# Seven block products for eight in the r and z gates, and partial results seeded into PSUM

## The chip, the core and the metric

The kernel runs on one core of one Trainium2 chip. The metric is device time in microseconds, first to last instruction, as a median of several executions. The kernel works in float32. In this kernel's trace every float32 product appears as two matmul entries, so a count in the trace is twice the count in the code.

## The reference

64 graphs of 256 nodes with 256 features; `x` and `adj` are both (64, 256, 256). Cut to what matters:

```python
h = maximum(layernorm(x), 0)
out = x + layer(h, adj)

# layer(x, mask), d = 256
xc = transpose(x)
c = relu(bn(conv1d(xc, conv1_w)))                  # 1 tap
c = bn(conv1d(c, conv2_w, pad=8))                  # 17 taps
x_conv = transpose(relu(c + xc))
s = x @ w_se.T + b_se                              # 3 features
A = exp(-dist(s)) * mask
msg = relu(x @ w_msg.T + b_msg)
x_nmp = einsum('bnm,bmd->bnd', A, msg)
gi = concat([x_conv, x_nmp]) @ w_ih.T + b_ih       # 512 -> 3 * 256
gh = x @ w_hh.T + b_hh                             # 256 -> 3 * 256
r = sigmoid(gi_r + gh_r)
z = sigmoid(gi_z + gh_z)
n = tanh(gi_n + r * gh_n)
return (1 - z) * n + z * x
```

## The kernel before

Everything is kept transposed (channels on partitions). Two graphs form a *pair* (index `i`, 512 columns: two graphs of 256 nodes), four pairs form a *batch* of eight graphs. conv2 is done for a whole batch at once by a polynomial transform of length 16 along the nodes: VectorE makes the forward transform (`U`, `V`), TensorE multiplies each of 16 bins with its transformed filter (15 of them complex, three real products each), VectorE transforms back (`Yu`, `Yv`). The bins' filters are streamed from DRAM, 256 KB for each product. The rest is done pair by pair and is interleaved by hand; a small model (`pace`) decides where queued VectorE steps are put.

Tiles in PSUM, and one step of conv2 (two bins):

```python
def aux(): return psum.tile([P, W], FP, name="aux", bufs=3)     # W = 512: one bank
def acc(): return psum.tile([P, W], FP, name="acc", bufs=5)

def products(b, m, between=None):
    p = [acc() for _ in range(3)]
    for n in range(2):
        if n and between: between()
        for kind, v in enumerate(operands(2 * m + n)):
            ...                                   # 4 matmuls of 128 columns into p[kind]
            load_kind(b, 2 * m + n + 3, kind)     # filter, three bins ahead, 9 buffers
    p1 = work.tile([P, W], FP, name="p1")
    if m < 7:
        nc.scalar.copy(p1, p[0])
        nc.vector.tensor_sub(re, pv[0], pv[2])    # pv[0] is p1
        nc.vector.tensor_add(im, pv[0], pv[1])
    ...
```

From the features to the weighted adjacency of a pair:

```python
def message(i):
    for g in range(G):
        for c in range(MC):
            p = acc() if g * MC + c == 3 else aux()
            ...                                               # 2 matmuls of 259 columns
            nc.vector.tensor_add(MSG[i][:, g, c, :], p[:, :D + SE], b_msg)
    ...                                                       # ScalarE: four small ops into z
    for g in range(G):
        nc.scalar.activation(MSG[i][:, g, :, :D], MSG[i][:, g, :, :D], AF.Relu)

def embed(i):                                                 # z is transposed
    p = aux()
    for j in range(2):
        transpose(p[:, j * P:(j + 1) * P], Z[:, j].rearrange("p q s -> p (q s)"))
    nc.scalar.copy(ZT[:, :P], p[:, :P])
    ...                                                       # and eight copies of 32 x 128

def affinity(i):                                              # exp(-dist) * adj
    for g in range(G):
        for c in range(MC):
            p = acc() if q == 3 else aux()
            nc.tensor.matmul(p[:, :N], ZT[rows_q, :P], ZT[rows_q, P:], start=True, stop=True)
            nc.scalar.activation(E[i][:, g, c], p[:, :N], AF.Exp, scale=-1.0)
    ...                                                       # four VectorE products with adj
```

The gates, called twice for each pair (`dc` is the half of the 256 output channels):

```python
def gates(i, dc, wait=None, early=None):
    ...
    ghn = acc()
    product(ghn, h, n, True, True)
    nc.scalar.activation(gn, ghn, AF.Identity, bias=...)
    pr, pn, pz = acc(), acc(), acc()
    product(pr, h + xn, r, True, False)          # h: the pair itself, xn: aggregated messages
    if early: early()
    product(pn, xn, n, True, False)
    product(pz, h + xn, z, True, False)
    if wait: wait()
    product(pr, xc, r, False, True)              # xc: the convolution's result
    nc.scalar.activation(tr, pr, AF.Tanh, ...)
    nc.vector.scalar_tensor_tensor(gn, tr, 1.0, gn, op0=ALU.add, op1=ALU.mult)
    product(pn, xc, n, False, True)
    nc.vector.scalar_tensor_tensor(gn, gn, 0.5, pn, op0=ALU.mult, op1=ALU.add)
    nc.scalar.activation(nn, gn, AF.Tanh, ...)
    product(pz, xc, z, False, True)
    nc.scalar.activation(tz, pz, AF.Tanh, ...)
    ...                                          # three VectorE steps: (1 - z) * n + z * h into d
```

Each `product` is two or four matmuls of 512 columns. `finish(i)` transposes `d` back, adds `x` and stores. The schedule of a batch, cut:

```python
    message(i); products(b, 0); embed(i); products(b, 1); affinity(i); products(b, 2)
    finish(i - 1); products(b, 3); aggregate(i); products(b, 4)
    message(i + 1)
    products(b, 5, lambda i=i: embed(i + 1))
    affinity(i + 1)
    join_h(nxt)                     # nxt: the same pair of the next batch; two ScalarE copies
    products(b, 6); products(b, 7)
    aggregate(i + 1)
    message(i + 2)
    gates(i, 0, wait, early)        # early: embed(i + 2); wait: affinity(i + 2), conv1(nxt)
    gates(i, 1, None, early)        # early: join_h(nxt + 1)
    conv1(nxt + 1); aggregate(i + 2)
    gates(i + 1, 0, lambda nxt=nxt: join_h(nxt + 2))
    conv1(nxt + 2); finish(i)
    gates(i + 1, 1)
    join_h(nxt + 3); message(i + 3); conv1(nxt + 3)
    gates(i + 2, 0, wait, lambda i=i: embed(i + 3))
    aggregate(i + 3); finish(i + 1)
    gates(i + 2, 1)
    gates(i + 3, 0); finish(i + 2); gates(i + 3, 1)
```

Of the kernel before, what the change touches and what calls it, by code (L numbers as in the profile page):

```python
# [42 lines left out]
class Fft:  # L43
# [160 lines left out]
    def p_back(self, Y, T):  # L204


        return [self.sub(T(0, 0), Y(0, 4), Y(1, 4)),
                self.sub(T(0, 2, 2), Y(0, 6, 2), Y(1, 6, 2)),
                self.add(Y(0, 4), Y(0, 4), Y(1, 4)),
# [71 lines left out]
def filter_points(bins, taps):  # L281


    cols = []
    for n in bins:
        z = [(ROOTS[n] if n < 15 else 1.0) ** (taps - 1 - t) for t in range(taps)]
        if n < 15:
            cols += [[v.real for v in z], [v.imag - v.real for v in z], [v.real + v.imag for v in z]]
        else:
            cols += [[1.0] * taps, [(-1.0) ** (taps - 1 - t) for t in range(taps)]]  # L290
    return np.array(cols, np.float64).T
# [10 lines left out]
def kernel(  # L302
# [221 lines left out]
    def aux():  # L524
        return psum.tile([P, W], FP, name="aux", bufs=3)

    def acc():
        return psum.tile([P, W], FP, name="acc", bufs=5)
# [5 lines left out]
    def columns(name):  # L534
        t, n = ROWS[name]
        k = sum(n)
        p = aux()
        nc.tensor.transpose(p[:, :k], t, ident[:k, :k])
        c = const.tile([P, k], FP, name=f"{name}_columns")
        nc.vector.tensor_copy(c, p[:, :k])  # L540
        return [c[:, sum(n[:j]):sum(n[:j + 1])] for j in range(len(n))]
# [80 lines left out]
    def transpose_h(i):  # L622
        if i >= B // G:
            return
        HT[i] = work.tile([P, DC, W], FP, name="hT", bufs=6)
        for dc in range(DC):
            p = aux()
            for j in range(G * MC):
                transpose(chunk(p, j // MC, j % MC), X[i][:, j, dc * P:(dc + 1) * P])
            if i == 0:  # L630
                nc.vector.tensor_scalar(HT[i][:, dc, :], p, 0.0, None, ALU.max)
            else:
                nc.scalar.activation(HT[i][:, dc, :], p, AF.Relu)  # L633
# [41 lines left out]
    def conv1(i, other=acc):  # L675
        if i >= B // G:
            return
        for o in range(DC):
            p = acc() if o == 0 else other()
            for k in range(DC):  # L680
                mm(p, w_c1[:, k, o * P:(o + 1) * P], HT[i][:, k, :], W, start=(k == 0), stop=(k == DC - 1))
            v = h1.rearrange("p (g o) s b -> p o g s b", o=DC)[:, o, :, :, 1:1 + NW]
            u = p.rearrange("p (g s b) -> p g s b", g=G, b=NW)
# [23 lines left out]
    def filters(m, g, eng):  # L707
# [3 lines left out]
        p = acc()  # L711
        for dc in range(DC):
            mm(p[:size * kinds, dc * D:(dc + 1) * D], points[m][:size * TAPS, :size * kinds],
               taps[:size * TAPS, g, dc, :], D, start=True, stop=True)
# [6 lines left out]
    WB = {}  # L721

    def load_kind(b, n, kind):
        b, n = b + n // BINS, n % BINS
        if b < NB and (n < BINS - 1 or kind < 2):
            WB[b, n, kind] = work.tile([P, DC, D], FP, name="wb", bufs=9)
            m = n // len(PASSES[0])
            nc.sync.dma_start(out=WB[b, n, kind], in_=filt[m][:, 3 * (n - PASSES[m][0]) + kind])  # L728

# [14 lines left out]
    def products(b, m, between=None):  # L744
        p = [acc() for _ in range(3)]
        for n in range(2):
            if n and between:
                between()
            for kind, v in enumerate(operands(2 * m + n)):
                if v is None:  # L750
                    load_kind(b, 2 * m + n + 3, kind)
                    continue
                for o in range(DC):
                    for k in range(DC):
                        mm(p[kind][:, (n * DC + o) * P:(n * DC + o + 1) * P],
                           WB[b, 2 * m + n, kind][:, k, o * P:(o + 1) * P],
                           v[:, k::DC, 0, :], P, start=(k == 0), stop=(k == DC - 1))
                load_kind(b, 2 * m + n + 3, kind)
        p1 = work.tile([P, W], FP, name="p1")
        pv = [t.rearrange("p (n a e) -> p a n e", n=2, e=NW) for t in (p1, p[1], p[2])]  # L760
        if m < 7:
            nc.scalar.copy(p1, p[0])
            if m < 4:
                re, im = Yv(m % 2, m // 2 * 2, 2), Yv(m % 2, 4 + m // 2 * 2, 2)
            elif m < 6:
                re, im = Yu(m - 4, 0, 2), Yu(m - 4, 2, 2)
            else:
                t = Yu.t[:, :, :, 6:8, :].rearrange("p a c n e -> p n a c e")
                re, im = t[:, 0], t[:, 1]
            pace.vector(2 * W, pace.pe + PSUM)  # L770
            nc.vector.tensor_sub(re, pv[0], pv[2])
            nc.vector.tensor_add(im, pv[0], pv[1])
        else:
            half = W // 2
            nc.scalar.copy(p1[:, :half], p[0][:, :half])
            nc.scalar.mul(Yu(0, 4)[:, :, 0, :], p[0][:, half:].rearrange("p (a e) -> p a e", e=NW), 0.5)
            nc.scalar.mul(Yu(1, 4)[:, :, 0, :], p[1][:, half:].rearrange("p (a e) -> p a e", e=NW), 0.5)
            pace.vector(W, pace.pe + PSUM)
            nc.vector.tensor_sub(Yu(0, 5)[:, :, 0], pv[0][:, :, 0], pv[2][:, :, 0])
            nc.vector.tensor_add(Yu(1, 5)[:, :, 0], pv[0][:, :, 0], pv[1][:, :, 0])  # L780
# [11 lines left out]
    def message(i):  # L792
        MSG[i] = work.tile([P, G, MC, D + SE], FP, name="msg")
        for g in range(G):
            for c in range(MC):
                p = acc() if g * MC + c == 3 else aux()
                for k in range(DC):
                    mm(p[:, :D + SE], chunk(HT[i][:, k], g, c), w_msg[:, k, :], D + SE,
                       start=(k == 0), stop=(k == DC - 1))
                pace.vector(D, pace.pe + PSUM)  # L800
                nc.vector.tensor_add(MSG[i][:, g, c, :], p[:, :D + SE], b_msg)
# [11 lines left out]
    def embed(i):  # L813
        p = aux()
        for j in range(2):
            transpose(p[:, j * P:(j + 1) * P], Z[:, j].rearrange("p q s -> p (q s)"))
        nc.scalar.copy(ZT[:, :P], p[:, :P])
        for q in range(G * MC):
            for c in range(MC):
                m = q // MC * MC + c  # L820
                nc.scalar.copy(ZT[q * Q:(q + 1) * Q, (1 + c) * P:(2 + c) * P], p[m * Q:(m + 1) * Q, P:2 * P])


    def affinity(i):
        E[i] = work.tile([P, G, MC, N], FP, name="e")
        for g in range(G):
            for c in range(MC):
                q = g * MC + c
                p = acc() if q == 3 else aux()
                rows_q = slice(q * Q, q * Q + KD)  # L830
                nc.tensor.matmul(p[:, :N], ZT[rows_q, :P], ZT[rows_q, P:], start=True, stop=True)  # L831
                nc.scalar.activation(E[i][:, g, c], p[:, :N], AF.Exp, scale=-1.0)
# [10 lines left out]
    def transpose_a(i):  # L843
        AT[i] = late.tile([P, 2 * MC, W], U16, name="adjh").bitcast(FP).rearrange("p a (b n) -> p a b n", n=N)
        AT[i] = AT[i].rearrange("p a b n -> p (a b) n").rearrange("p (g c) n -> p g c n", g=G)
        for g in range(G):
            q = aux()
            for c in range(MC):
                for r in range(MC):
                    transpose(q[:, c * N + r * P:c * N + (r + 1) * P], E[i][:, g, r, c * P:(c + 1) * P])  # L850
            nc.scalar.copy(AT[i][:, g].rearrange("p c n -> p (c n)"), q)

    def aggregate(i):
        XNM[i] = late.tile([P, DC, W], FP, name="xnm", bufs=2)
        for dc in range(DC):
            p = aux()
            for g in range(G):
                for c in range(MC):
                    mm(graph(p, g), MSG[i][:, g, c, dc * P:(dc + 1) * P], AT[i][:, g, c, :], N,
                       start=(c == 0), stop=(c == MC - 1))  # L860
            nc.scalar.activation(XNM[i][:, dc, :], p, AF.Copy)
# [3 lines left out]
    OT = {}  # L865

    def gates(i, dc, wait=None, early=None):
        h = [(w_hh[:, k], HT[i][:, k, :]) for k in range(DC)]
        xn = [(w_ih[:, DC + k], XNM[i][:, k, :]) for k in range(DC)]
        xc = [(w_ih[:, k], xcv(i % PB, k)) for k in range(DC)]  # L870

        def product(p, terms, row, first, last):
            for j, (w, r) in enumerate(terms):
                mm(p, w[:, row:row + P], r, W, start=first and j == 0, stop=last and j == len(terms) - 1)

        r, z, n = dc * P, D + dc * P, 2 * D + dc * P
        ghn = acc()
        product(ghn, h, n, True, True)
        gn = late.tile([P, W], FP, name="gn")
        nc.scalar.activation(gn, ghn, AF.Identity, bias=b_hh[:, 2 * DC + dc:2 * DC + dc + 1])  # L880
        pr, pn, pz = acc(), acc(), acc()
        product(pr, h + xn, r, True, False)
        if early:
            early()
        product(pn, xn, n, True, False)
        product(pz, h + xn, z, True, False)
        if wait:
            wait()
        product(pr, xc, r, False, True)
        tr = late.tile([P, W], FP, name="tr")  # L890
        nc.scalar.activation(tr, pr, AF.Tanh, bias=b_rz[:, dc:dc + 1], scale=0.5)  # L891
        pace.vector(W, pace.pe + ACT)
        nc.vector.scalar_tensor_tensor(gn, tr, 1.0, gn, op0=ALU.add, op1=ALU.mult)  # L893
        product(pn, xc, n, False, True)
        pace.vector(W, pace.pe + PSUM)
        nc.vector.scalar_tensor_tensor(gn, gn, 0.5, pn, op0=ALU.mult, op1=ALU.add)  # L896
        nn = late.tile([P, W], FP, name="nn")
        nc.scalar.activation(nn, gn, AF.Tanh, bias=b_ih[:, 2 * DC + dc:2 * DC + dc + 1])  # L898
# [286 lines left out]
```

## Time and profile before

| what | value |
|---|---|
| time, median of 3 | 1829.45 us (1827.57 to 1829.56) |
| gate matmuls with xnm, hT and Yv, 128x512 | 3 x 768 entries |
| conv2's matmuls, 128x128, with V, U, Sv, PT | 1024, 1024, 512 and 448 entries |
| VectorE subtract and add of conv2 (L771, L772, 128x512) | 22.0 + 21.8 + 16.4 + 16.4 us |
| ScalarE copy p<-acc (L762) | 32.9 us, 587 ns each |
| mean granted TensorE clock | 0.995 |

How to read the profile: PE is TensorE's matmuls and PEld its weight loads, DVE is VectorE, ACT is ScalarE, POOL is GpSimd. A line `DVE gn L893 <- ACT tr L891: 209.5, 34, 11.9` says that VectorE sat idle before line 893 until ScalarE's line 891 was done, 209.5 us in 34 times, at most 11.9 at once. The chain of work that ended last goes back from the last instruction, at each step to what released it. In a timeline, an entry gives start, length, engine, line, operation and count, and in brackets the idle time before it. Idle time of an engine that isn't the bottleneck costs nothing.

### The profile page before, as it was taken

How to read it: one execution, taken by the hardware profiler on the slowest of the kernel's cores; microseconds unless marked ns; L12 is line 12 of the kernel's file. 1: busy time of each engine (PE TensorE's matmuls, PEld its weight loads, DVE VectorE, ACT ScalarE, POOL GpSimd, SP SyncE). 2: the span in 40 equal slices, each digit the busy share in tenths (PEclk: the TensorE clock that was granted, in tenths of full speed). 3: DMA queues.
4: the chain of work that ended last, by engine and by line, in shares of the span. 5: the costliest groups of instructions: out<-in, count | busy, mean ns of one | idle time of the engine just before them, and what ended most of it. 6: DMA issues, size and time to landing. Idle time of an engine off the chain costs nothing.

```text
span 1828.3 us, 21930 instructions
## 1 busy us (share of the span) xinstructions
PE 1793.1 (98%) x7462; PEld 1110.8 (61%) x7462; DVE 1366.6 (75%) x2596; ACT 765.4 (42%) x1508; POOL 219.2 (12%) x357
## 2 busy tenths in 40 slices
PE   5999999999999999999999999999999999999998
PEld 3787454964569544784448645595546944487453
DVE  4789669794879849797697967888587984979422
ACT  2535532364333643265422653246432463225321
POOL 2211002101111011111012000110111110111000
PEclk9999999999999999999999999999999999999999
DMA  7788543854438444565347644494544744164011
GB/s 195 230 272 216 125 105 88 242 144 114 109 95 258 101 106 93 154 198 116 84 99 215 171 91 110 86 263 119 114 102 118 224 106 95 42 185 116 8 40 34
DMA packets 250483, 245.96 MB, mean 135 GB/s; under 512 B 142936, under 2 KB 176500, under 8 KB 250371
## 3 DMA queue, kind: packets, MB, share of 16 engines
q1 hardware_dynamic: 216634, 183.83, 37.0%
q0 software_dynamic: 30784, 58.07, 14.1%
q10 hardware_dynamic: 2953, 2.66, 0.7%
q8 instruction: 59, 0.97, 0.2%
q14 instruction: 53, 0.43, 0.1%
HBM read 156.56 MB, written 44.30 MB: 110 GB/s over the span
## 4 chain that ended last, share of the span: by engine, by line
PE 94%; issue 2%; DMA 2%; DVE 1%; POOL 1%; ACT 0%; SPq 0%; POOLq 0%; ACTq 0%
PE acc L517 80%; PE aux L517 11%; PE aux L521 2%; PE aux L831 1%; DMA x<-in_x_dram 1%; DMA filt<-fo 1%; DMA wb<-filt 0%; POOL filt L717 0%; POOL rstd L565 0%; DVE st L559 0%; ACT fo L716 0%; SPq L728 0%; POOL bn_scale L595 0%; DVE Sv L571 0%; DVE y L926 0%
## 5 line engine op out<-in xcount | busy, mean ns | idle before, releaser
L517 PE MATMUL acc<-xnm,w_ih 128*128 128x512 f32 x768 | 353.1, 592 | 0.0
L517 PE MATMUL acc<-hT,w_hh 128*128 128x512 f32 x768 | 350.5, 592 | 0.0
L517 PE MATMUL acc<-Yv,w_ih 128*128 128x512 f32 x768 | 342.7, 596 | 1.9 <-ACT Yv L789 1.9
L517 PEld LDWEIGHTS acc<-Yv,w_ih 128*128 128x128 f32 x768 | 145.8, 191 | 185.4 <-issue 180.9
L517 PEld LDWEIGHTS acc<-xnm,w_ih 128*128 128x128 f32 x768 | 144.7, 190 | 176.0 <-issue 175.5
L517 PEld LDWEIGHTS acc<-hT,w_hh 128*128 128x128 f32 x768 | 143.9, 190 | 164.6 <-issue 152.6
L893 DVE SCALAR_TENSOR_TENSOR gn<-tr,gn 128x512 f32<-128x512 f32 x64 | 44.1, 689 | 209.6 <-ACT tr L891 209.5
L891 ACT ACTIVATE tr<-acc,b_rz 128x512 f32<-128x512 f32 x64 | 43.9, 686 | 344.6 <-PE acc L517 344.6
L927 POOL DMA_DIRECT2D out_dram<-y x62 | 38.3, 622 | 785.0 <-DVE y L926 760.0
L517 PE MATMUL acc<-V,wb 128*128 128x128 f32 x1024 | 124.8, 275 | 0.0
L517 PE MATMUL acc<-U,wb 128*128 128x128 f32 x1024 | 124.3, 276 | 0.0
L517 PEld LDWEIGHTS acc<-U,wb 128*128 128x128 f32 x1024 | 120.0, 192 | 3.6 <-DVE T L59 2.0
L59 DVE SCALAR_TENSOR_TENSOR V<-T,V 128x256 f32<-128x256 f32 (+2 forms) x224 | 121.8, 613 | 0.3
L517 PEld LDWEIGHTS acc<-V,wb 128*128 128x128 f32 x1024 | 119.5, 192 | 0.0
L517 PE MATMUL acc<-hT,w_c 128*128 128x512 f32 x228 | 107.4, 612 | 2.3 <-ACT hT L633 1.4
L517 PE MATMUL aux<-e,msg 128*128 128x256 f32 x464 | 104.9, 379 | 0.0
L898 ACT ACTIVATE nn<-gn,bn_columns 128x512 f32<-128x512 f32 x64 | 46.3, 724 | 129.8 <-DVE gn L896 129.8
L517 PEld LDWEIGHTS aux<-e,msg 128*128 128x128 f32 x464 | 87.1, 190 | 17.7 <-issue 6.9
L565 POOL TENSOR_TENSOR rstd<-rstd,neg_half 128x4 f32<-128x4 f32 x32 | 38.0, 1188 | 477.4 <-DVE shift L567 373.6
L517 PE MATMUL aux<-w_msg,hT 128*128 128x259 f32 x384 | 89.5, 382 | 0.0
L517 PEld LDWEIGHTS aux<-w_msg,hT 128*128 128x128 f32 x384 | 72.2, 190 | 17.2 <-issue 7.2
L426 ACT COPY adj<-adjh 128x1024 uint16<-128x1024 uint16 x58 | 74.0, 1346 | 18.6 <-DMA adjh<-halves_d 18.6
(164 smaller groups left out, 2731.0 us busy)
## 6 DMA issues: line engine op xcount, KB each, us to landing
wb<-filt SPq DMA_DIRECT2D x376, 256.0 KB
y<-in_x_dram POOLq DMA_DIRECT2D x64, 256.0 KB, 5.5
out_dram<-y POOLq DMA_DIRECT2D x62, 256.0 KB, 5.7
x<-in_x_dram SPq DMA_DIRECT2D x60, 256.0 KB
halves_d<-halves SPq DMA_DIRECT2D x116, 128.0 KB
adjh<-halves_d POOLq DMA_DIRECT2D x116, 128.0 KB, 5.8
hh<-halves SPq DMA_DIRECT2D x108, 128.0 KB
filt<-fo POOLq DMA_DIRECT2D x18, 252.0 KB, 5.5
```

The lines of the kernel that those rows point to most:

```text
L59: return self.step(out, lambda: self.v.scalar_tensor_tensor(out, x, s, y, op0=ALU.mult, op1=ALU.add))
L426: nc.scalar.copy(v[:, j], u[:, j])
L517: nc.tensor.matmul(p, w, v, **kw)
L521: nc.tensor.transpose(p, v, ident)
L565: nc.gpsimd.tensor_tensor(t["rstd"], t["rstd"], neg_half, ALU.pow)
L831: nc.tensor.matmul(p[:, :N], ZT[rows_q, :P], ZT[rows_q, P:], start=True, stop=True)
L891: nc.scalar.activation(tr, pr, AF.Tanh, bias=b_rz[:, dc:dc + 1], scale=0.5)
L893: nc.vector.scalar_tensor_tensor(gn, tr, 1.0, gn, op0=ALU.add, op1=ALU.mult)
L898: nc.scalar.activation(nn, gn, AF.Tanh, bias=b_ih[:, 2 * DC + dc:2 * DC + dc + 1])
L927: eng.dma_start(out=rows(out, G * i + g), in_=row_tile(Y[i], g))
```

## The change

Before, a gate's 256 x 256 weights times a pair's 256 channels is done in blocks of 128 x 128: for each of the three inputs and each half of the pair, eight block products. The change takes the two halves of the pair (the two graphs) as the columns of a 2 x 2 block matrix and uses a seven-product scheme. For it the weights' sums are made once (`w_x`), the inputs' sums for every pair on VectorE (`sums_a`, `sums_b`), and the partial results are combined in PSUM: ScalarE or VectorE writes a partial result into a bank, and later matmuls accumulate onto it. In conv2's complex products the shared real product is copied into a second bank by ScalarE, and the other two are accumulated onto the two copies, so that VectorE's subtract and add fall away. For these combinations every PSUM tile has two banks, two buffers for each of the two names. The order of the batch is rearranged around this. The diff, cut to its core:

```diff
-        return psum.tile([P, W], FP, name="aux", bufs=3)
+        return psum.tile([P, 2, W], FP, name="aux", bufs=2)
-        return psum.tile([P, W], FP, name="acc", bufs=5)
+        return psum.tile([P, 2, W], FP, name="acc", bufs=2)
...
+    def begin(m):
+        p = OPEN[m] = acc()
+        for n in (2 * m, 2 * m + 1):
+            product(p[:, 0], n, 0, n % 2 == 0)
+        nc.scalar.copy(p[:, 1], p[:, 0])
+    def complete(m):
+        p = OPEN.pop(m)
+        for kind in (1, 2):
+            for n in (2 * m, 2 * m + 1):
+                if operands(n)[kind] is not None:
+                    product(p[:, 2 - kind], n, kind, False)
+        ...                                     # ScalarE copies both banks out
...
     def affinity(i):
+        banks = [aux() for _ in range(G)]
...
+    def gates(i, late_xc=None, after5=None, fill=None, after7=None, after4=None, after=None):
+        A = acc()
+        if late_xc:                             # the first pair of a batch
+            part(A[:, 0], 1, i, IN[:2], True)
+            E5 = acc()
+            part(E5[:, 1], 5, i, IN[:2], True)
+            gn = ghn(i)
+            late_xc()
+            part(A[:, 0], 1, i, IN[2:])
+        else:
+            part(A[:, 0], 1, i, IN, True)
+            E5 = acc()
+        nc.scalar.mul(E5[:, 0], A[:, 0], -1.0)
+        part(E5[:, 1], 5, i, IN[2:] if late_xc else IN, not late_xc)
+        nc.scalar.copy(e, E5[:, 1])
+        if after5: after5()
+        part(A[:, 0], 2, i)
+        part(E5[:, 0], 6, i)
+        nc.vector.tensor_add(A[:, 1], E5[:, 0], e)
+        if not late_xc: gn = ghn(i)
+        if fill: fill()
+        part(E5[:, 0], 7, i)
+        nc.vector.scalar_tensor_tensor(E5[:, 1], E5[:, 0], -1.0, e, op0=ALU.mult, op1=ALU.subtract)
+        if after7: after7()
+        part(A[:, 1], 3, i)
+        open_gates(A, 0)                        # two tanh on ScalarE
+        part(E5[:, 0], 4, i)
+        open_gates(E5, 1)
+        if after4: after4()
+        nc.vector.scalar_tensor_tensor(gn, tr, 1.0, gn, op0=ALU.add, op1=ALU.mult)
+        Gn = acc()
+        ...                                     # n gate as before: 8 matmuls of 512 columns
+        nc.vector.scalar_tensor_tensor(gn, gn, 0.5, Gn, op0=ALU.mult, op1=ALU.add)
+        ...                                     # two tanh on ScalarE
+        if after: after()                       # the next pair's input sums
+        ...                                     # the blend, four VectorE steps
```

`part` is one block product for both gates: six matmuls of 256 columns. The weights' nine buffers of conv2 hold the gates' input sums between two uses. The batch after, cut:

```diff
-        products(b, 4)
-        message(i + 1)
-        products(b, 5, lambda i=i: embed(i + 1))
+        begin(4)
+        begin(5)
+        message(i + 1)
+        complete(4)
+        complete(5)
+        embed(i + 1)
         affinity(i + 1)
...
         message(i + 2)
+        embed(i + 2)
+        conv1(nxt)
+        turn_h(nxt + 1)                         # four ScalarE steps into hh
+        affinity(i + 2)
+        sums_a(i, "h")
+        sums_a(i, "xn")
+        gates(i, late_xc, after5, fill, None, None, after)
         conv1(nxt + 1)
         aggregate(i + 2)
+        gates(i + 1, None, lambda: finish(i), fill, None, None, after)
         conv1(nxt + 2)
+        message(i + 3)
         join_h(nxt + 3)
+        embed(i + 3)
         conv1(nxt + 3)
+        affinity(i + 3)
+        gates(i + 2, None, lambda: finish(i + 1), fill, None, lambda: aggregate(i + 3), after)
+        gates(i + 3, None, lambda: finish(i + 2), lambda: join_adj(nxt), after7, after4)
```

`fill` of the first two pairs holds `join_h` of the next batch's pairs 1 and 2, `fill` of the first three their `turn_h`. Messages are added, affinities exponentiated and results finished two banks at a time.

## The prediction

> **What bounds the kernel now.** I read the page first, then the list of waits, then the timeline of single engines. The first lines of the page give the answer:
>
> ```profile
> span 1828.3 us, 21930 instructions
> PE 1793.1 (98%) x7462; PEld 1110.8 (61%) x7462; DVE 1366.6 (75%) x2596; ACT 765.4 (42%) x1508; POOL 219.2 (12%) x357
> PE 94%; issue 2%; DMA 2%; DVE 1%; POOL 1%; ACT 0%; SPq 0%; POOLq 0%; ACTq 0%
> ```
>
> TensorE works 98% of the span and makes up 94% of the chain that ended last. In the list of waits, filtered to TensorE, only these lines come from after the start-up:
>
> ```profile
> PE aux L521 <- DVE d L915: 2.9, 2, 1.5
> PE acc L517 <- ACT Yv L789: 1.9, 1, 1.9
> ```
>
> (Columns: total us, how often, longest.) So the order of work is such that TensorE is never kept waiting, and one batch of eight graphs (four pairs of two) takes 215.6 us of solid matmul: in the chain, the same piece starts at 1011.60 and at 1227.20. Any matmul removed is time gained, but any wait added is time lost one for one.
>
> Rates of one batch's stretch, TensorE timeline (start, length, count; one fp32 product stands as two entries, so counts are twice those of the code):
>
> ```profile
> 1067.79 3.62 PE L517 MATMUL aux<-e,msg 128*128 128x256 f32 x16
> 1071.25 3.60 PE L517 MATMUL acc<-hT,w_hh 128*128 128x512 f32 x8
> 1074.68 3.60 PE L517 MATMUL acc<-xnm,w_ih 128*128 128x512 f32 x8
> ```
>
> From start to start: 16 entries of 256 columns take 3.46 us (0.216 each), 8 of 512 take 3.43 (0.429 each). Halving the columns costs nearly nothing.
>
> The followers of one `message`, from the timelines of VectorE and of ScalarE:
>
> ```profile
> 1108.78 1.09 DVE L801 TENSOR_TENSOR msg<-aux,b_msg 128x259 f32<-128x259 f32 x3
> 1110.16 0.43 DVE L801 TENSOR_TENSOR msg<-acc,b_msg 128x259 f32<-128x259 f32 x1 [0.30 <-PE acc L517]
> ```
>
> ```profile
> 1107.30 2.55 ACT L671 COPY hT<-hh 128x1024 uint16<-128x1024 uint16 x2
> 1110.62 0.22 ACT L804 ACTIVATE z<-msg 128x12 f32<-128x12 f32 x1 [0.77 <-DVE msg L801]
> 1111.06 1.14 ACT L809 ACTIVATE msg<-msg 128x512 f32<-128x512 f32 x2
> 1119.17 2.17 ACT L821 COPY zT<-aux 32x128 f32<-32x128 f32 x8
> ```
>
> `z` is ready only 1.2 us after the message matmuls end, and `zT` 2.3 us after the transposes of `z`. Nobody feels it here: those transposes stand at 1118.59, between gate products, 8 us after `z` was ready, and `hT` was joined before `message`.
>
> **What the Trainium skill says.** "TensorE: Matmul & The Clock Gate", section "Architectural detail": TensorE runs its matmuls in order, and ScalarE and VectorE are strict first-in-first-out queues. The traces agree: in before, every late result is explained by what stands ahead of it. The same page, section "Why this matters for your kernels", warns of idle gaps over about 3 us in TensorE, after which its clock falls to half. The trace shows it once, in the start-up (table of windows: window, length, busy PE, PEld, DVE, ACT, POOL, clock, DMA):
>
> ```profile
> 40.00:50.00 10.00, 7.81 (x15) 3.89 (x16) 7.00 (x21) 3.80 (x7) 4.93 (x7) 0.51 0.58 181
> ```
>
> This followed a wait of 4.07 us; the eight transposes and the conv1 after it took 2.30 and 6.62 us where the next pair's took 1.04 and 3.70: 4.2 us lost. "PSUM — Partial Sum Buffer", section "The four PSUM rules", says that a matmul without the start flag adds to what ScalarE or VectorE wrote where an earlier matmul has set the bit; the seeding rests on this, no time does. The trace of before has no seeding.
>
> **What the change removes.** Before, each pair needs 36 products of 512 columns in the gates: 72 entries, 30.9 us (two times 15.45 in the chain). After: seven block products x three inputs x two gates = 42 products of 256 columns, 84 entries x 0.216 = 18.2 us, and the n gate as before, 24 entries x 0.429 = 10.3. That is 28.5, so 2.4 us less for a pair, **78 us for 32 pairs**. conv2 keeps its matmuls (same count, 128 columns, 0.112 each).
>
> **What it adds beside the path.** VectorE: sums of inputs (three of 512, six of 256: 3 x 0.69 + 6 x 0.37 = 4.3 us) and two PSUM combinations (1.4) for a pair, 182 us; it loses conv2's subtract and add (77 us by their four 512-wide rows) and some fixed costs by 1024-wide steps (1.22 instead of 1.37). About 1450 us of work, not a bound. ScalarE gets some 100 us of copies, to 870. Neither engine becomes the bound by its sum.
>
> **What it moves, and this decides.** The built order of after shows TensorE with less between a producer and its user. PSUM is four two-bank tiles instead of eight of one bank, so work can be interleaved less. I followed one middle batch by hand down the three queues, with the durations above and from the groups (512-wide VectorE step 0.66 to 0.69, 256-wide 0.34, 1024-wide 1.2; ScalarE seed 0.6, exp of two banks' halves 0.6, hh 0.52, relu of h 0.78, join 1.28). "Blend" is the last three-stage mix of a pair (1.2 + 2 x 0.66 + 1.2 = 3.75 us); times count from the end of a pair's n-gate matmuls, Gn. TensorE waits, per batch:
>
> 1. Batch start. `message` (3.5) and two `begin` (3.6) end at 7.1; VectorE does gn 1.2, five short steps 1.7, blend 3.75, two message adds 1.4, ScalarE z 0.5: z at about 8.8. Then the first `complete` waits for a seed that stands behind two relus (1.1 + 0.6). With some backlog of VectorE: 4.2 us.
> 2. Pair 1: z transposes and affinity now touch. ScalarE has two copies (1.2) and zT (2.3) first: 3.5.
> 3. Seed for bins 12 and 13 behind exps and a join of hT (2.6): 1.1.
> 4. Pair 2: z transposes directly behind `message`: at least 1.3; with conv2's last copies holding VectorE: 3.6.
> 5. First gate round. ScalarE from z on: relu 1.1, zT 2.3, two relus of h 1.6, scale 0.6, hh 2.1, exps 1.2 = 8.9; then the masks and the first input sum on VectorE, in front of which the join of conv2's parts waits for the same scale: 12 to 13. TensorE has z, conv1, affinity, block 1: 6.1. 6.6.
> 6. There block 7 follows block 6 with nothing between, and VectorE must read the bank: 1.0.
> 7. Gn of pair 1 needs the tile that the gate tanh reads, behind two joins and hh: 1.7.
> 8. Pair 3: z behind `message`: VectorE gn 1.2, sums 4.3, blend 3.75, message 0.7, ScalarE 0.5 = 10.5, against 6.9 of TensorE (conv1, message): 4.3 with the backlog.
> 9. conv1 behind it needs hT, which ScalarE joins after z's relus: 1.1 + 2.6, and affinity a free tile: 4.4.
> 10. Pair 3's gates: `finish` of pair 2 stands after blocks 1 and 5 (5.2), its blend ends at 1.2 + 4.3 + 3.75 = 9.3: 4.4 with small waits.
>
> Sum 34.8 us a batch against 9.7 saved (four pairs). The first batch lacks wait 1 but has the weight sums on VectorE, the last lacks the joins: I take 34 x 8 = 275. The tail gets about 3 us longer, as the last blend is not split by graph.
>
> 1829 - 78 + 275 + 3 = 2029. Waits 5, 8 with 9, and 10 or 1 are of the size that halved the clock in the start-up. Two such drops a batch, each some 3 us (the one seen cost 4.2; part of it hides a following wait): 16 x 3 = 48. **Predicted 2070 us**, 13% slower.
>
> **The rivals.** (a) *The gain comes through*: the waits are mostly hidden, as in before, and the time is 1829 - 78 + 10 to 30 = 1760 to 1780. For it: TensorE is at 98% and VectorE stays below 85%. Against it: waits 2, 5, 8, 9 and 10 follow from the order of the queues alone and come to over 20 us a batch even without any backlog. (b) *Waits without the clock*: gaps stay below what drops it: about 2030. (c) *Weight loads of conv2 become the bound*: the nine slots are shared with the gates' sums, and the queue can refill only from the last gate on; before, the conv2 stretch already moves 263 GB/s. For: seven slots filled at the start. Against: filling begins some 15 us ahead, and a stretch lengthened by waits asks less per us. It would add 20 to 60 us on top.
>
> **Range and chances.** If only the waits that the order forces (about 26 us a batch) are paid, 1829 - 78 + 208 + 3 = 1962; with every wait, four clock drops a batch and some late weights, about 2150. Range 1965 to 2150. Faster by over 2% needs fewer than 5 us of waits a batch, which I can't see: 0.05; within 2%: 0.04; slower: 0.91.
>
> **What would show it.** Right: TensorE's busy share falls to about 80 to 85%, its waits name z, zT, hT and the gates' input sums (wb), each some 8 times for 2 to 7 us, and slices with a clock below 0.9 appear; gate matmuls fall by 78 us. Wrong: TensorE stays above 95%, or the waits name wb<-filt. The estimate fails most easily if ScalarE's or VectorE's items are ready earlier than the order suggests, or if gaps of 4 us don't lower the clock.

## The result and the profile after

The changed kernel takes 2221.4 us (median of 4 runs, 2217.0 to 2226.0) against 1829.0 for the kernel before: a ratio of 1.214, 95% interval 1.212 to 1.217. It is slower, as predicted, but by 392 us where 241 were predicted, and 2221 lies above the range.

The page of the changed kernel, in the lines that were shown of before, and the row of granted clock (tenths of full speed in 40 slices; before it has 9 in every slice):

```profile
span 2219.6 us, 24339 instructions
...
PE 1902.7 (86%) x8614; PEld 1393.1 (63%) x8614; DVE 1443.3 (65%) x2599; ACT 852.3 (38%) x1600; POOL 219.0 (10%) x357
...
PEclk9979898999999899998989999999999989899988
...
PE 11%; DVE 3%; ACT 2%; issue 0%; ACTq 0%; DVEq 0%
```

TensorE's share has fallen from 98 to 86%, yet its busy time has *grown* by 110 us although matmul columns were taken out. Both happen at once: it waits, and it runs slower. (The chain's shares add up to 16% only: it breaks off, so I read the waits instead.)

TensorE's waits in the changed kernel (total us, how often, longest). Before had two such lines after the start-up, 2.9 and 1.9 us:

```profile
PE aux L520 <- ACT z L834: 44.6, 23, 7.3
PE aux L516 <- ACT h L687: 37.2, 28, 2.0
PE aux L520 <- DVE tr L1074: 30.9, 9, 6.6
PE acc L516 <- DVE wb L937: 29.0, 8, 4.6
PE aux L516 <- ACT gn L1002: 24.9, 32, 0.8
PE acc L516 <- ACT acc L1018: 22.5, 32, 0.7
PE aux L516 <- ACT hT L670: 21.9, 7, 3.1
PE acc L516 <- ACT fo L714: 16.1, 15, 4.2
```

`z`, `tr`, `wb` and `hT` are the waits of the prediction. `h`, `gn` and `acc L1018` are not in it: short waits, but 28 or 32 of them, about one per pair. Nor is `fo`, of the filters' transform, whose waits all lie in the start-up.

The table of windows, cut where the first conv2 product starts, of before and then of the changed kernel (columns as in the prediction):

```profile
105.36:1828.30 1722.94, 1712.09 (x7143) 1055.92 (x7142) 1300.68 (x2454) 721.07 (x1420) 191.55 (x304) 1.00 0.51 129
```

```profile
145.50:2219.60 2074.10, 1805.35 (x8295) 1336.85 (x8294) 1369.11 (x2438) 805.58 (x1513) 189.73 (x301) 0.93 0.39 107
```

These two lines split the loss. The start-up is 145.5 - 105.4 = 40.1 us longer. In the body TensorE stands idle for 2074.1 - 1805.35 = 268.8 us (33.6 a batch) where it was 10.9: +257.9. It is busy for 1805.35 - 1712.09 = 93.3 us more. 40.1 + 257.9 + 93.3 = 391.3, the difference of the two profiled spans.

Why busier? TensorE's timeline of the changed kernel (start, length, engine, line, operation, count, wait before it):

```profile
1002.67 0.54 PE L520 MATMUL aux<-ident,z 128*128 128x128 f32 x2 [1.84 <-ACT z L834]
1003.04 2.82 PE L516 MATMUL aux<-hT,w_c 128*128 128x512 f32 x4
1006.90 3.78 PE L516 MATMUL aux<-hT,w_c 128*128 128x512 f32 x4 [1.03 <-ACT h L687]
...
1018.78 3.78 PE L516 MATMUL acc<-wb,w_x 128*128 128x256 f32 x8 [4.61 <-DVE wb L937]
...
1051.43 1.88 PE L516 MATMUL aux<-hT,w_c 128*128 128x512 f32 x4
```

The same four entries of conv1 take 1.88 us at 1051 and 3.78 at 1006: twice as long, the half clock. The windows of the same stretch (columns as above, the third figure from the right is the granted clock) show it switching:

```profile
1000.40:1003.80 3.40, 1.56 (x6) 0.71 (x6) 3.15 (x6) 2.95 (x10) 2.35 (x4) 1.00 0.25 56
1003.80:1010.60 6.80, 5.77 (x7) 1.51 (x5) 0.00 (x0) 2.94 (x11) 0.00 (x0) 0.50 0.18 50
1010.70:1014.10 3.40, 3.17 (x16) 1.96 (x16) 2.02 (x4) 3.38 (x7) 0.00 (x0) 1.00 0.00 0
```

In this batch the granted clock falls to half five times, at 983.4, 1003.8, 1017.5, 1106.2 and 1160.9 us, for 3.4 to 10.2 us each. At half clock TensorE takes twice as long, so half of that busy time is lost: summed over the trace's record of the granted clock, 118.6 us in the body of the changed kernel and 1.9 in that of before.

What follows a `message` in the changed kernel, from VectorE's and ScalarE's timelines, against the lines of before:

```profile
1001.57 0.69 DVE L830 TENSOR_TENSOR msg<-aux,b_msg 128x518 f32<-128x518 f32 x1
```

```profile
1002.29 0.21 ACT L833 ACTIVATE z<-msg 128x12 f32<-128x12 f32 x1 [0.45 <-DVE msg L830]
1003.91 2.12 ACT L850 COPY zT<-aux 32x128 f32<-32x128 f32 x8
```

Each step is no slower than before. But the transposes of `z` now stand right behind the `message`, and TensorE waits for the whole of it (the 1.84 us above).

### The profile page after: what moved, and what is told of

Its sections match the earlier page's. It is cut to its first block, busy times and chain, and to the rows that moved or that the text cites. A ratio compares the mean times of both kernels' runs of the same rounds, so it can differ in the third digit from the quotient of the medians.

```text
span 2219.6 us, 24339 instructions
## 1 busy us (share of the span) xinstructions
PE 1902.7 (86%) x8614; PEld 1393.1 (63%) x8614; DVE 1443.3 (65%) x2599; ACT 852.3 (38%) x1600; POOL 219.0 (10%) x357
## 3 DMA queue, kind: packets, MB, share of 16 engines
q0 software_dynamic: 30784, 58.07, 10.2%
## 5 line engine op out<-in xcount | busy, mean ns | idle before, releaser
L516 PE MATMUL acc<-wb,w_x 128*128 128x256 f32 x768 | 195.1, 405 | 58.4 <-DVE wb L937 29.0
L516 PEld LDWEIGHTS acc<-wb,w_x 128*128 128x128 f32 x768 | 149.4, 200 | 109.5 <-ACT acc L1018 36.2
L516 PE MATMUL acc<-xnm,w_ih 128*128 128x512 f32 (+1 forms) x512 | 206.8, 508 | 6.4 <-ACT wb L1044 6.4
L516 PE MATMUL acc<-Yv,w_ih 128*128 128x512 f32 (+1 forms) x512 | 201.1, 498 | 8.0 <-ACT Yv L818 8.0
L516 PE MATMUL aux<-hT,w_c 128*128 128x512 f32 x224 | 150.1, 806 | 59.1 <-ACT h L687 37.2
L1002 ACT ACTIVATE gn<-aux,bn_columns 128x512 f32<-128x512 f32 x64 | 44.0, 687 | 334.1 <-PE aux L516 334.1
L516 PE MATMUL aux<-hT,w_hh 128*128 128x512 f32 x256 | 128.4, 626 | 24.9 <-ACT gn L1002 24.9
L868 DVE TENSOR_TENSOR e<-e,adj 128x256 f32<-128x256 f32 x128 | 67.9, 593 | 109.3 <-ACT e L862 109.2
L516 PEld LDWEIGHTS aux<-hT,w_c 128*128 128x128 f32 x224 | 50.1, 242 | 138.3 <-ACT h L687 70.1
L516 PE MATMUL acc<-wb,w_ih 128*128 128x256 f32 x512 | 131.4, 379 | 0.0
```

The costliest lines, as they stand in the source:

```text
L516: nc.tensor.matmul(p, w, v, **kw)
L868: nc.vector.tensor_mul(e, e, ADJ[i][:, g * MC + c].rearrange("p (b h c) -> p c h b", c=MC, b=NW))
L1002: nc.scalar.activation(gn[:, dc], p[:, dc], AF.Identity, bias=b_hh[:, 2 * DC + dc:2 * DC + dc + 1])
```

## The experiments

Theories. **A**: the loss is waits of the moved order plus the half clock that they bring. **B**: the two-bank tiles make waits of their own. **C**: the seven-product chain (input sums, seeds, combinations) costs by itself more than it saves. Times are medians; the kernel before ran beside each, 1828.4 to 1829.5 us.

### 1. Dummy matmuls in the waits

```diff
+    def warm(p, n):                # n products of 512 columns, results overwritten
+        for _ in range(n):
+            nc.tensor.matmul(p, w_c1[:, 0, :P], w_c1..., start=True, stop=True)
+        warm(...)                  # ahead of embed, affinity, conv1 of pair 3, finish, block 5
```

> The changed kernel with 18 products a batch added that nobody reads (17 in the first batch, 15 in the last): each writes 512 columns of a PSUM bank that is overwritten next, placed just ahead of the long TensorE waits (z of pairs 0, 2 and 3, zT of pair 1, hT of the next batch's pair 3, the first gate round's input sums, finish of pair 2). They take 0.86 us each where TensorE would idle. Theory 'waits drop the clock' (the clock falls because TensorE idles for 2 to 5 us within a short time): the granted clock rises from 0.93 to 0.97 or more, the product entries that ran at half speed speed up, and although more work is done the time falls by 70 to 150 us, to 2070 to 2150 us. Rival 'the clock falls for another reason' (narrower products, seeded banks): clock stays near 0.93, and the time stays at 2221 or rises by up to 60 us.

Measured: 2150.6 us (ratio 1.175, 1.173 to 1.177), clock 0.982 for 0.929, at the upper end of the first range. The 140 dummy products are 140 x 2 x 0.429 = 120 us of added matmul, in place of which 100 us of idle time went (317 to 216): alone, that would make the kernel 20 us slower. It is 71 us *faster*, as TensorE's busy time rose by 25 us only. Some 95 us of half clock went (by the record of the granted clock 118.6 - 22.6 = 96), which shows it as a cost of its own, beside the waits.

### 2. One-bank tiles, same order

```diff
-        return psum.tile([P, 2, W], FP, name="aux", bufs=2)
+        return Pair("aux")         # two tiles [P, W], name "aux", bufs=4; acc alike
```

ScalarE and VectorE then read each bank with an instruction of its own where they read two at once.

> The two-bank PSUM part undone alone: every tile has one bank, four buffers for each of the two names (the same eight banks), and the operations that spanned two banks are split (message add, exp, gate tanh, n-gate sum, result sum). Order unchanged. Theory 'a wait is for the tile, not for the bank' (TensorE filling the second bank waits for ScalarE reading the first one): the waits for h L687 (37 us), gn L1002 (25 us), the seed L1018 (22 us) and fo L714 (25 us, in the filters) go nearly to zero, the first conv2 product starts at about 105 to 120 us instead of 145, and with somewhat fewer clock drops the time is 2040 to 2120 us. Rival 'those waits are for engines that are late anyhow': they move to the next user, the time is above 2180 us.

Measured: 2058.5 us (1.125, 1.124 to 1.127), 163 less. The waits for `gn` and `acc L1018` are gone, those for `h` and `fo` down from 41.6 and 25.3 us to 2.1 and 1.6; the waits of the order stay:

```profile
PE aux L520 <- ACT z L846: 51.0, 23, 6.9
PE acc L516 <- DVE wb L952: 30.0, 7, 4.6
```

The first conv2 product starts at 107.7 us, so the start-up's loss was the tiles' too. B holds. With a tile of two banks, TensorE did not fill the second bank until ScalarE had read the first: conv1, the hidden part of n, the filters, all waited like that.

### 3. Another order, two-bank tiles kept

```diff
-        message(i); ...; embed(i)          # at the batch's start
+        message(nxt)                       # ahead of pair 3's n gate, one batch earlier
-        complete(5); embed(i + 1)
+        embed(i + 1); complete(5)
-        embed(i + 2); conv1(nxt); ...; affinity(i + 2); sums_a(...)
+        conv1(nxt); embed(i + 2); sums_a(...)   # affinity and turn_h inside the gates, behind ghn
-        message(i + 3); join_h(nxt + 3); embed(i + 3)
+        message(i + 3)                     # ahead of pair 1's n gate; embed behind it
```

and `finish` of pair 2 ahead of pair 3's block 7, where it stood behind block 5.

> The order alone, two-bank tiles kept: message of the next batch's pair 0 and of pair 3 stand ahead of an n gate, z of pair 1 is transposed between two complete, pair 2's z comes after conv1 and its affinity after ghn, the first input sums stand ahead of the masks, pair 3's hT joins follow zT, and finish of pair 2 follows ghn. Theory 'the order of the queues makes the waits' (items 1, 2, 4, 5, 8, 9, 10 of the prediction, measured at 145 us in all, and the clock drops that follow them, some 120 us): time 1940 to 2020 us, clock above 0.97. Rival 'the seven-product chains themselves are too long' (waits reappear at the seeds and PSUM combinations): above 2100 us.

Measured: 2094.0 us (1.144, 1.139 to 1.149), 127 less. The size was missed: the waits for `z` and `zT` nearly went (44.6 to 1.8, 18.0 to 3.1 us), but conv1 now stands where its tile is still being read (`h` 57.5 us for 37.2), and the input sums still come late (`wb`, 29.0 us as before). Waits at the seeds, which the rival expected, did not grow (`acc L1018` 22.5 us, here 17.8).

### 4. Both

> One-bank tiles and the new order together. If the two causes are the whole of it, TensorE's waits after the start-up fall below 40 us, the clock is above 0.99 and the 78 us of removed gate work come through: 1770 to 1830 us. If VectorE becomes the bound in conv2's stretch, waits for its results remain: 1850 to 1950 us.

Measured: 1915.0 us (1.047, 1.045 to 1.048), 306 less; 163 + 127 = 290 was what the two gave singly. The time is inside the second range, but its reason is seen only in part: of the three largest waits left, one is for VectorE.

```profile
PE aux L516 <- ACT hT L681: 35.1, 7, 5.0
PE acc L516 <- DVE wb L952: 21.3, 13, 2.9
PE acc L516 <- ACT Yv L829: 20.0, 8, 8.3
```

### 5 and 6. Plain eight products, in two-bank and in one-bank tiles

```diff
-        part(A[:, 0], 1, i, ...) ... part(E5[:, 0], 4, i)      # seeds, sums, combinations
+        both(A, 0, IN, True, True)         # r, z of the first half: 512 columns, 6 terms each
+        both(E5, 1, IN, True, True)        # the second half
```

> The changed kernel with its two-bank tiles, order and seeded conv2, but with r and z gates as plain sums of eight block products again: 512-column products, no sums of inputs, no weight sums, no seeds and no combinations in the gates. It has 78 us more of matmul columns at full clock than the changed kernel (9.7 a batch). It loses the waits for the input sums and for the combinations (4.6 + 0.9 us a batch, 44 in all) and the clock drop that follows the first of them (8 us at half clock, 4 us a batch, 32 in all). Theory (tiles and order hold the loss, the seven-product chain only a small part): 2221 + 78 - 44 - 32 = 2223, say 2170 to 2270, with TensorE still idle 25 us a batch or more. Rival (the seven-product chain with its seeds, sums and combinations is what costs): back to 1850 to 1950.

> Plain eight products in r and z as in the run with eight products, and every two-bank tile split into two tiles of one bank: what is left of the change is conv2's seeding and the new order of the parts. Theory (the bank tiles cost some 160 us whatever the gates do): 160 less than the run with eight products, 2010 to 2110, so that order and conv2's seeding still cost over 180 against the kernel before. Rival (with one-bank tiles and plain gates nothing that costs is left): 1830 to 1880.

Measured: 2136.1 us (1.165, 1.160 to 1.170) and 1985.2 us (1.085, 1.083 to 1.088). Both lie under the theory's ranges: the tiles' cost of some 160 us is confirmed by another pair (151), but in the changed order eight products are 85 and 73 us *faster* than seven. I had counted 76 us of waits and clock as going with the chain. In two-bank tiles it was 317 - 218 = 99 us of TensorE's idle time, and its busy time rose by 19 us only where 78 of columns were added: some 59 us of slower running went too, 45 of them half clock by the record of the granted clock. So C is right where the chain is not covered. What costs is not only the first wait for sums: `tr` and `z` behind them are earlier as well (30.9 to 6.7, 44.6 to 34.5 us), presumably as VectorE has no input sums ahead of the blend and of the messages.

### 7. The waits of run 4, one by one

```diff
+        sums_a(i, "h"); sums_a(i, "xn")    # ahead of message(i + 2), not behind
+            pace.flush(joined[0])          # conv2's last relu ahead of ghn
+            late_xc()                      # ahead of affinity(i + 2), not behind
-        part(A[:, 0], 2, i); part(E5[:, 0], 6, i); tensor_add(...)
+        part(E5[:, 0], 6, i); tensor_add(...); part(A[:, 0], 2, i)
+        def after4(): conv1(nxt + 1)       # ahead of pair 0's n gate
+        def after5(): conv1(nxt + 3); finish(i + 1)    # in pair 2's gates
```

> One-bank tiles and the changed order of the fourth run (1915 us), and six more moves for the waits that its trace still shows, 11.4 us a batch: sums of h and xn ahead of the message of pair 2; conv2's last relu ahead of the hidden part of n on ScalarE; the affinity behind the first round's sums; block 6 ahead of block 2; conv1 of the next batch's pair 1 ahead of pair 0's n gate; conv1 of pair 3 into pair 2's gates (its wait of 5.0 us a batch). Theory (waits, and the half clock that they bring, are all that is left): 8 or 9 of the 11.4 us go, 64 to 72 in all, and most of two clock drops a batch of some 4 us each, up to 60: 1790 to 1850, clock at 0.98 or more. Rival (VectorE, 76% busy, sets the pace of these stages, and a wait only moves to its next result): 1880 to 1915.

Measured: 1837.2 us (1.004, 1.003 to 1.005), clock 0.984: 78 less, inside the first theory's range; A holds for these places.

### 8. Four more places

```diff
+        if late_xc: affinity(i + 2); turn_h(i + PB + 1)    # behind block 5's copy
-        def after4(): conv1(nxt + 1)
+        def after4(): turn_h(nxt + 2)                      # conv1(nxt + 1) behind the n gate again
+        begin(6); begin(7); join_h(nxt)                    # join behind the seeds
```

> The previous run (1837 us, one-bank tiles and the new order) with the four places mended where its TensorE still waits in nearly every batch: conv1 of the next batch's pair 1 back behind pair 0's n gate (it waited 1.3 to 2.3 us for hT), that pair's next normalised rows behind the tanhs on ScalarE (1.4 us), the affinity and the rows of the next pair behind block 5's copy (1.0 us), the join of hT behind conv2's last seeds (0.8 us). Theory (what is left over the saving in the gates is these waits): 4.5 to 5.4 us a batch in seven or eight batches, 32 to 43 us: 1790 to 1808, under the kernel before by 1 to 2%. Rival (the waits only move on along ScalarE's and VectorE's order): 1820 to 1840.

Measured: 1856.7 us (1.016, 1.013 to 1.018), 20 *more*. The rival was right, and worse. ScalarE's timeline, then TensorE's:

```profile
857.08 2.52 ACT L681 COPY hT<-hh 128x1024 uint16<-128x1024 uint16 x2 [12.70 <-DMA hh<-halves]
...
861.31 0.81 ACT L1064 ACTIVATE tr<-acc,b_rz 128x256 f32<-128x256 f32 x2
```

```profile
862.53 3.51 PE L516 MATMUL acc<-xnm,w_ih 128*128 128x512 f32 x4 [5.72 <-ACT wb L1064]
```

The join of `hT` stands still on ScalarE until its transfer lands, and the tanhs behind it, which free the tile for the n gate, stand with it. It was so in run 7 too, but there conv1 lay between them and the n gate.

### 9. Run 8 with plain eight products

> The mended kernel with r and z as plain sums of eight block products: no sums of inputs, no weight sums, no seeds and combinations in the gates; tiles, order and conv2 as in the mended kernel. Theory (the seven products bring their 78 us once their own waits are hidden, and cost only while something waits): 70 to 80 us longer than the mended kernel, 1860 to 1885. Rival (the chain of seven costs more than it saves whatever the order, as in the two pairs of runs before, where eight products were 73 and 85 us faster): 1720 to 1800.

Measured: 1864.5 us (1.019, 1.017 to 1.020), 8 more than run 8. Its TensorE waits for 13 us in all from 150 us on:

```profile
span 1863.4 us, 21580 instructions
...
PE 1817.4 (98%) x7462; PEld 1122.4 (60%) x7462; DVE 1276.2 (68%) x2362; ACT 817.2 (44%) x1635; POOL 219.6 (12%) x357
```

The range of the theory was met, its difference (70 to 80) was not, as run 8 had 43 us of new waits.

### 10. Run 8's two new waits moved

```diff
-        if late_xc: affinity(i + 2); turn_h(i + PB + 1)    # behind block 5's copy
+        if late_xc: turn_h(i + PB + 1)
+        if late_xc: affinity(i + 2)                        # behind block 2
-        def fill(): join_h(nxt + 1)                        # ahead of the tanhs
+        def after4(): join_h(nxt + 1); turn_h(nxt + 2)     # behind them
```

> The mended kernel (1857 us) showed two new waits in every batch where its mends had put others: up to 5.9 us ahead of pair 0's n gate, because the join of hT stood ahead of the tanhs on ScalarE and waited for its transfer, and 2.1 us ahead of block 7, because VectorE masked the affinity first. Here the join stands behind the tanhs, and the affinity behind block 2; nothing else is changed. Theory (only these waits and the half clock behind them are left): 15.1 + 27.6 us of waits go, and some 10 to 30 us of half clock: 1780 to 1808, 1 to 2.5% under the kernel before, clock at 0.985 or more. Rival (they move on once more): 1830 to 1860.

Measured: 1810.7 us (0.989, 0.988 to 0.991). **1.1% faster than the kernel before**, 3 us past the expected range, clock 0.981 where 0.985 was expected. The page, the one wait left in most batches, and it in two batches:

```profile
span 1809.3 us, 24557 instructions
...
PE 1747.1 (97%) x8614; PEld 1347.7 (74%) x8614; DVE 1453.7 (80%) x2726; ACT 880.3 (49%) x1827; POOL 219.3 (12%) x357
```

```profile
PE acc L516 <- DVE acc L1044: 10.6, 7, 2.0
```

```profile
832.25 2.86 PE L516 MATMUL acc<-wb,w_x 128*128 128x256 f32 x12 [1.68 <-DVE acc L1044]
1041.47 4.52 PE L516 MATMUL acc<-wb,w_x 128*128 128x256 f32 x12 [1.68 <-DVE acc L1044]
```

Busy time in the body: 1662 us, where 1712 - 78 = 1634 would be as in before; by the record of the granted clock 21.5 of the 28 us between them are half clock.

### 11. VectorE's addition first

```diff
-        pace.vector(W, pace.pe + PSUM)     # lets queued conv2 steps run first
+        pace.vector(W)
         nc.vector.tensor_add(A[:, 1], E5[:, 0], e)
```

> The kernel of 1811 us with one line changed: VectorE's addition of block 6 and the copied block 5, for which TensorE still waits 1.7 us in seven of eight batches and then runs 1.7 us longer at half clock in six of them, is put ahead of the conv2 steps that stood before it; TensorE's own order is unchanged. Theory: 10.6 us of waits and some 10 us of half clock go: 1786 to 1800, clock at 0.99. Rival (VectorE then stands still until block 6 is done and is late elsewhere): 1808 to 1830.

(Five of the waits were followed by half clock, not six.) Measured: 1842.2 us (1.007, 1.005 to 1.008), 31 more: the rival, and 12 above its range. VectorE's timeline of this run and TensorE's:

```profile
838.95 0.70 DVE L1044 TENSOR_TENSOR acc<-acc,wb 128x512 f32<-128x512 f32 x1 [1.77 <-PE acc L516]
...
850.80 0.70 DVE L1054 SCALAR_TENSOR_TENSOR acc<-acc,wb 128x512 f32<-128x512 f32 x1
```

```profile
851.55 1.22 PE L516 MATMUL acc<-wb,w_hh 128*128 128x256 f32 x2 [4.10 <-DVE acc L1054]
```

VectorE stood still 1.77 us for block 6, then had the postponed conv2 steps ahead of the next combination, for which TensorE waits 4.1 us. A wait of 1.7 became one of 4.1.

## Why the prediction was wrong

The sum's terms were -78 + 275 + 3 + 48 = +248 (rounded down to 2070). Against them stands the measured +391:

- **Gates, -78: right.** Entries of 256 columns run at 0.216 us where the clock is full. In the ordered kernels, body busy time is 1731 us with eight products (run 9) and 1662 with seven (run 10): 69, although the second loses 15 us more at half clock (21.5 for 6.1 by the record of the granted clock).
- **Waits, 34.8 a batch: the sum right, its parts not.** 33.6 measured. In the batch that I followed, the ten places come to only about 21 us: the largest are 4.61 (predicted 6.6, the first round's sums), 3.13 (4.4, `hT`), 3.04 (4.4, `finish`); the seed for bins 12 and 13 doesn't wait at all (1.1). The missing part, some 11 to 12 us, is a kind of wait that I didn't see: the second bank of a tile behind ScalarE's read of the first, 0.7 to 1.6 us each. I wrote that two-bank tiles mean "work can be interleaved less" and followed it up only where a whole tile is needed; run 2 shows what it costs. Two errors cancelled, by luck.
- **"Two such drops a batch, each some 3 us": the step that failed.** Five drops in the batch that I counted, and 117 us of half clock in the body (118.6 - 1.9) against 48. I allowed it only for waits of 4 us and more, after the one in the start-up of before. Waits of 1.6 to 2 us did it too, and before showed that already: I wrote that its trace has the drop once, but its granted clock is at half for 3.4 us from 1688.8 as well, and from 1821.9 to its end. The first follows the wait of 1.9 us for `Yv` that I had printed:

```profile
1688.56 5.83 PE L517 MATMUL acc<-Yv,w_ih 128*128 128x512 f32 x9 [1.89 <-ACT Yv L789]
```

Nine such entries take 4.0 us at full clock (0.429 from start to start). Run 1 took some 95 us of half clock away by filling waits with dummy work alone.
- **Other busy time: not in the sum.** Busy time is 93.3 us over before where -78 was due: 171, of which 117 are half clock. Of the other 54, some 30 go with the waits: ahead of a wait, the last entry counts at its full length (four of 512 columns: 1.88 us, where without a wait the next begins after 1.72), and from 150 us on TensorE waits 188 times, in before 3 times. What makes the rest is not known.
- **The start-up: not in the sum.** 40 us, by the `filters`, whose two results share a tile; with one-bank tiles 38 of them are gone (145.5 to 107.7).
- **Tail, +3: 5.5.** From the end of the last gate matmul to the end of the span it is 10.4 us in before, 15.9 in the changed kernel. This lies inside the idle and busy time above; no run isolates its cause.

So 391 - 248 = 143 us were missed: 69 of half clock, 54 of other busy time and 40 of start-up, less 17 of waits (257.9 net for 275) and the 3 of the tail, which these contain. My rival (c), late conv2 weights, didn't come: no run's waits name `wb<-filt`. "Faster by over 2%" was to need "fewer than 5 us of waits a batch": run 10, with 37 us idle in the body (4.7 a batch), meets that by order and tiles alone and is 1.1% faster, with half clock still in it.

On the drops the prediction used the Trainium skill, "TensorE: Matmul & The Clock Gate", section "Why this matters for your kernels", which speaks of gaps over about 3 us. The same page, "A second HAM failure mode: psum-queue depth-cycling", says that small idles between groups of matmuls, if frequent enough, make the clock swing. The traces agree with the second (9 of 66 waits of 1.6 to 2.0 us, in the table at the end), and I should have followed it.

What the change is worth is now this table (us):

```
tiles, order                        seven products   eight products
two-bank, order of the change            2221             2136
one-bank, order of the change            2058             1985
one-bank, order of run 8                 1857             1865
one-bank, order of run 10                1811              -
kernel before (own order and conv2)        -              1829
```

The seven products lose 73 to 85 us in the order of the change, where their sums and combinations are waited for. In the order of run 8 they win 8 us in spite of 43 us of such waits, and with most of these gone (run 10 against run 9) 54 us, of which a small part may be run 10's two moves. Run 9 is still 35 us over the kernel before, with the same block products in its gates. By the traces 5 of the 35 lie ahead of the first conv2 product, 3 behind the last gate matmul and the rest between them; whether conv2's seeding or the order causes them, no run tells apart, as the seeding was never taken out alone.

## What to carry to other kernels

On a kernel whose TensorE is 98% busy, fewer matmul columns pay only if each removed product doesn't put another engine's result between two matmuls: count such results and the work that covers each. A tile was one unit for waiting here, so two banks that are filled and read at different times belong in two tiles. And a wait on TensorE can cost its own length once more by halving the clock: 1.68 us of wait brought 1.66 us of slower matmuls in run 10, and in the changed kernel 269 us of idle time brought 119.

## What the hardware showed that I had not expected

How long a wait of TensorE must be to halve the clock, over the changed kernel and the eleven runs, from 150 us on. Counted are groups of four or more entries over 128 rows that begin after a wait, transposes left out; slow means over 1.35 times the full-speed length (1.88 us for four of 512 columns):

```
wait ahead, us     groups   slow
0.2 to 1.6            436     44
1.6 to 2.0             66      9
2.0 to 3.0             31     17
over 3.0               83     82
```

(Slow ones after the shortest waits lie partly in stretches that were slow already. Of 30 groups of transposes behind waits over 3 us, two ran at full speed.) The length of the wait sets no sharp threshold, and the same place goes both ways, as the two lines of run 10 show: 1.68 us ahead of both, 2.86 and 4.52 us long.

What decides is where the wait falls. The Trainium skill's page on the clock gate, section "What's actually happening", tells of a window of about 3.4 us that runs free of the kernel's work, and the traces show it: in all thirteen, from 150 us on and short of the last 20 us, the 478 changes of the granted clock lie within 0.06 us of a grid of 3.41 us, whose offset from the kernel's start differs from run to run (0.1 to 3.1 us). For each step of this grid I took the share of it in which TensorE is busy by the profile, without the affinity's matmuls over 9 rows. From full clock, half clock followed after 203 of 204 steps that were less than 40% full, 34 of 138 between 40 and 55%, and 1 of 6097 above. From half clock, full clock came back after 228 of 228 steps over 82% full and 1 of 129 under 78%. If the matmuls over 9 rows are counted as busy, 65 of the 238 drops follow steps over 55% full in place of that one: in these traces they do not hold the clock up. Run 10's first wait ran over the edge of two steps, 72 and 59% full; the second fell into one, 32% full, behind the affinity's 0.7 us.
